# Patch transfers of sixteen channels, read-back in 4 KB pieces and a new order of work in an attention and expert-convolution kernel

## The chip, the cores and the metric

The kernel runs on one core of a Trainium2 chip. Its time is the device time of one launch in microseconds. A core has five engines with an instruction queue each, which run in order and wait for one another through semaphores: TensorE (PE, with its weight loads as PEld), VectorE (DVE), ScalarE (ACT), GpSimd (POOL) and SyncE (SP). SyncE issues nearly all transfers here; 16 DMA engines carry them out.

## The reference

The input x has 16 images of 256 channels and 64 x 64 pixels, in float32. Two residual layers follow one another.

```
h   = groupnorm(x)
q,k,v = w_qkv @ rmsnorm(h)              # 4 heads of 32
ctx = softmax_tokens(k) @ v^T           # 32 x 32 per head, over 4096 tokens
y   = x + rmsnorm(w_out @ (ctx @ softmax_channels(q)) + b_out)

h2  = groupnorm(y)
p   = softmax(router(mean(h2)) / 2)     # 4 experts, the best 2 per image
out = y + sum over the 2 experts e of
      p_e * (pw_e @ gelu(depthwise3x3_e(h2) + dw_b_e) + pw_b_e)
```

The gelu is the exact one, and pw_e is a 256 x 256 pointwise convolution. The experts differ per image, so each image's filters and pointwise weights are fetched after its routing.

## The kernel before

An image is cut into 8 groups of 512 tokens for the attention layer, and into 4 quarters of 16 rows (2 halves of 32) for the expert layer. Several images are in work at once: while image b is in its depthwise and pointwise stage, image b+1 goes through its output stage, and image b+2 is read and projected. "The next image" and "the one after" below mean these.

**The order.** `pipelined_path` writes all the work of the 16 images as rows, each a small function such as `out_norm(b, g, hf)` or `conv0(b, h, t)` with a place in time. The place is a start, plus a slot per group, plus an offset from a dictionary called PLAN of about 3,100 entries, in which a name such as "tap16@e1.2" overrides the common offset for certain images and groups. The rows are sorted by place (L1648) and emitted in that order under `tc.manual_schedule()` (L1649). So every engine's queue holds its instructions in the order of the rows; no scheduler moves them after that.

**The attention stage.** `turn_x` transposes tokens (PE, tile px), `x_keep` copies them scaled out of PSUM (ACT or DVE, tile xt), `project` makes q and k (PE, pq), `evacuate` takes the exponentials (ACT, e), `context` accumulates the contexts (PE, pc). Later `attend` computes the outputs (PE, po), `out_sq` their squares (ACT, junk), `out_norm` writes them scaled as tile ob (DVE at L1183, some on ACT at L1181), `out_turn` transposes ob (PE, tr, L1188), and `out_add` adds the result to the image in SBUF (DVE, ring, L1197).

**The expert stage.** Channels 128 to 255 are convolved on VectorE: `start1` on ACT (L1467), eight `tap1` on DVE (acc, L1474, 128 x 1024 each), `gelu1` on ACT (L1482). Channels 0 to 127 go through TensorE. `pad0` writes a padded half into pd; `lay` stores it to HBM (L1380); `spread` reads patches of it back into a tile xr, in which each partition holds one input row at one horizontal shift, for a block of 8 channels (L1393 and L1397); `conv0` multiplies them with banded filter tables (PE, dw, L1432), two calls `conv0(2v)` and `conv0(2v+1)` filling the same two PSUM banks. `gelu0` takes both banks to SBUF (ACT, hx, L1444), `put` stores them to HBM with channels and rows exchanged (L1449), and `take` reads them back with channels on partitions as tile hp (L1460). `pointwise` multiplies acc and hp with the experts' weights (PE, pw, L1503), `residual` adds the result to the image (DVE, ring, L1518), and `store` writes it out (L1521).

**Buffers.** There are four xr tiles of 8 channels, used in turn, three hx, three acc and one hp. PSUM's banks for dw, pw, px, tr and the others are handed out in turn in the order of the rows, so each first write to a bank waits for the last reader of its former contents.

Of the kernel before, what the change touches and what calls it, by code (L numbers as in the profile page):

```python
# [16 lines left out]
P = 128  # L17
# [7 lines left out]
NE = 4  # L25
# [25 lines left out]
NXR = 4  # L51
# [9 lines left out]
    "load_x1": 2.02, "mean": 1.19, "means": 13.36, "dev": 13.73, "devs": 17.34, "scale": 17.85,  # L61
    "bias": 21.91, "in_lead": 26.39, "norm0": -8.96, "norm1": -3.87, "turn_x0": 0.72, "x_sq0": 1.77,
    "x_sq1": 2.31, "turn_x1": 1.43, "x_sq2": 3.45, "x_sq3": 3.25, "token": 4.42, "x_keep0": 5.53,
    "x_keep1": 5.77, "x_keep2": 5.97, "x_keep3": 6.03, "project0": 3.18, "evacuate0": 6.05,
    "project1": 3.64, "evacuate1": 6.46, "project2": 3.67, "evacuate2": 6.47, "project3": 4.06,
    "evacuate3": 6.58, "context": 9.48, "q_sum": 8.22, "q_norm": 11.06, "q_turn": 14.73,
    "q_keep": 16.31, "mix_a": 9.53, "mix_turn": 10.09, "mix_v": 11.08, "mix_vv": 11.63,
    "mix_b": 11.82, "mix_out": 13.35, "mix_c": 13.91, "mix_lead": 16.02, "attend0": -1.14,
    "out_sq0": -0.04, "out_sq1": 0.35, "out_scale0": 0.42, "out_norm0": 1.58, "attend1": -0.28,
    "out_sq2": 1.31, "out_sq3": 1.37, "out_scale1": 3.18, "out_norm1": 4.28, "out_turn0": 5.64,  # L70
    "out_add0": 6.51, "sq_sums0": 8.92, "out_turn1": 6.16, "out_add1": 7.06, "sq_sums1": 9.17,
    "sums1": 9.6, "means1": 9.77, "scale1": 10.52, "router": 10.97, "route": 11.89, "choose": 13.68,
    "pick_taps": 21.03, "route_lead": 21.97, "weigh": 29.78, "pick_bias": 41.15, "pad1": -10.35,
    "start0": -0.53, "tap01": 1.33, "tap02": 1.57, "tap03": 1.59, "tap04": 1.87, "tap05": 2.54,
    "tap06": 4.55, "tap07": 4.74, "tap08": 6.14, "gelu10": 13.51, "start1": 1.94, "tap11": 3.52,
    "tap12": 8.13, "tap13": 8.14, "tap14": 8.54, "tap15": 9.95, "tap16": 12.84, "tap17": 13.06,
    "tap18": 14.42, "gelu11": 15.46, "pw00": 16.32, "pw01": 16.45, "pw02": 17.78, "pw03": 17.83,
    "pw10": 16.09, "pw11": 16.24, "pw12": 19.85, "pw13": 20.43, "residual00": 19.8,
    "residual01": 20.37, "store0": 32.19, "residual10": 22.5, "residual11": 23.44, "store1": 26.19,
    "in_first": 0.96, "in_more": 1.71, "q_first": 3.46, "out_first": 27.07, "out_more": 37.75,  # L80
    "q_less": 0.19, "load_a0": -17.62, "load_a1": -6.91, "load_b0": -15.96, "load_b1": -6.67,
    "stats0": -13.55, "stats1": -1.94, "load_weights": 58, "scale_weights": -7.03,
    "end_pw00": 135.48, "end_pw01": -49.35, "end_pw02": 69.96, "end_pw03": 337.87,
    "end_residual00": 3.29, "end_residual01": 66.1, "end_pw10": 115.56, "end_pw11": -47.98,
    "end_pw12": -196, "end_pw13": -114.87, "end_residual10": -13.43, "end_residual11": 88.85,
    "x_0": 0.99, "x_1": -0.21, "x_2": -0.19, "x_e1": 5.09, "x_e2": 4, "route_0": -3.83,
    "route_1": 0.32, "route_2": -0.55, "route_e1": -1.2, "route_e2": -0.21, "out_0": -5.81,
    "out_1": -0.4, "out_2": 0.09, "out_e1": -1.85, "out_e2": -0.87, "q_0": -7.21, "q_1": -2.22,
    "q_2": 0.4, "q_e1": -1.65, "q_e2": -0.57, "in_0": -22.93, "in_1": 7.98, "in_2": 2.65,
    "in_e1": -1.58, "in_e2": 0.28, "pw04": -112.48, "pw14": -23.18, "x_last": 16.71,  # L90
    "v_last": 15.93, "v_e1": 3.4, "tap18@e2.3": 12.73, "start0@e1.3": -0.55, "x_sq2@2.2": 2.88,
    "gelu11@e1.2": 17.06, "tap03@0.1": 1.97, "project0@0.0": 2.01, "out_norm1@2.7": 4.71,
    "out_sq1@e2.0": 0.64, "out_scale1@1.2": 2.19, "evacuate0@1.2": 5.17, "context@1.7": 8.38,
    "out_scale1@0.0": 4.74, "q_norm@0.0": 15.63, "out_turn0@1.4": 5.23, "token@2.1": 4.75,
    "project0@2.7": 3.47, "context@0.7": 8.6, "attend1@e1.3": -2.08, "out_norm1@1.1": 3.87,
    "context@2.1": 7.79, "q_norm@0.6": 12.94, "out_norm0@1.1": 1.4, "gelu11@e2.3": 13.29,
    "evacuate2@1.7": 6.62, "out_norm1@0.6": 4.18, "evacuate2@2.2": 6.81, "project0@2.3": 4.02,
    "token@2.2": 4.19, "norm0@0.0": -14.16, "q_sum@0.0": 10.99, "x_sq2@2.6": 2.62,
    "norm1@0.0": -4.28, "out_norm1@e1.1": 5.78, "x_sq2@1.2": 2.18, "tap04@e2.2": 2.29,
    "x_keep0@0.5": 6.43, "out_turn0@1.2": 5.58, "evacuate3@1.7": 8.13, "x_sq2@2.5": 2.77,  # L100
    "turn_x0@0.0": -3.93, "out_scale0@1.2": 2.15, "tap13@2.0": 6.26, "x_keep3@1.2": 6.99,
    "out_turn0@1.3": 4.82, "q_sum@e2.6": 8.44, "x_sq2@0.0": -1.29, "scale1@0.0": 11.1,
    "token@0.1": 2.33, "q_sum@1.5": 10.67, "q_sum@1.1": 7.71, "tap12@e1.1": 3.08,
    "x_keep1@0.1": 3.76, "evacuate2@1.6": 5.71, "q_sum@1.3": 8.05, "route@0.0": 12.55,
    "x_sq2@1.4": 2.43, "q_turn@0.2": 15.05, "bias@0.7": 26.53, "token@1.4": 3.4,
    "pick_taps@e1.0": 23.22, "out_add0@2.5": 6.36, "means@0.7": 10.61, "dev@e2.7": 6.55,
    "evacuate3@1.2": 6.52, "x_sq3@1.4": 3.12, "x_keep1@0.7": 6.49, "mix_v@0.7": 11.95,
    "token@1.1": 4.49, "tap17@e2.3": 11.87, "out_turn0@e1.1": 7.3, "token@0.2": 4.15,
    "q_sum@1.2": 9.02, "out_norm0@1.2": 4.52, "x_keep0@0.7": 6.45, "mix_b@e1.7": 12.79,
    "choose@1.0": 14.4, "project0@e1.7": 2.76, "tap07@e1.2": 8.15, "tap11@e1.2": 5.96,  # L110
    "means@1.7": 3.31, "token@1.3": 3.93, "q_sum@e1.6": 8.87, "tap12@e2.0": 8.3,
    "out_scale0@1.3": 2.06, "route@e1.0": 12.62, "pick_taps@2.0": 19.25, "out_turn0@1.0": 5.21,
    "scale@0.7": 20.54, "tap06@e1.0": 3.75, "out_turn1@e2.2": 8.74, "token@0.7": 3.73,
    "q_sum@e2.7": 9.96, "stats0@e2.5": -12.47, "out_turn0@1.5": 5.79, "token@1.6": 3.52,
    "q_turn@e2.1": 14.09, "out_norm1@e2.5": 4.67, "weigh@0.0": 26.02, "x_sq2@1.0": 3.24,
    "out_turn0@0.3": 5.99, "turn_x0@2.2": -1.78, "mix_b@0.7": 18.63, "out_scale1@e2.6": 2.5,
    "gelu11@e1.0": 17.52, "token@e2.7": 4.04, "context@1.2": 12.21, "q_sum@e2.0": 7.26,
    "tap01@e1.3": 1.63, "tap12@e2.2": 6.87, "x_sq2@1.6": 3.27, "load_a1@1.6": -5.34,
    "q_sum@0.1": 9.32, "q_sum@2.5": 8.88, "q_norm@0.2": 14.49, "tap13@e2.3": 7.37,
    "weigh@2.0": 30.01, "q_sum@e2.3": 12.37, "stats1@1.0": -3.82, "q_sum@1.0": 8.13,  # L120
    "project1@2.2": 5.8, "context@1.4": 11.54, "mean@1.7": -2.48, "tap03@e1.2": 2.37,
    "token@2.4": 4.54, "q_turn@e2.3": 15.48, "mix_b@1.7": 11.59, "out_sq3@e2.5": 1.73,
    "pick_bias@1.0": 35.23, "tap03@e1.3": 2.45, "out_norm1@0.7": 3.64, "choose@2.0": 14.28,
    "out_turn0@0.1": 5.13, "x_keep1@0.5": 6.47, "out_norm1@0.5": 4.68, "router@2.0": 11.05,
    "means1@e1.0": 10.29, "mean@0.7": 2.67, "project0@e2.7": 2.49, "x_keep0@1.7": 6.78,
    "context@1.3": 10.14, "router@0.0": 11.21, "tap17@e1.3": 13.61, "sq_sums1@0.7": 11.44,
    "x_sq1@1.4": 2.79, "x_keep0@1.1": 6.45, "context@0.4": 10.21, "project2@2.3": 0.53,
    "out_turn1@e1.6": 7.27, "project0@e1.5": 5.68, "turn_x0@e1.7": 0.11, "q_sum@e2.5": 11.2,
    "out_turn0@e1.6": 5.98, "out_turn0@e2.5": 5.25, "tap01@e1.2": -3.61, "evacuate3@0.0": 7.65,
    "tap02@e2.2": 1.4, "sq_sums1@e1.7": 7.95, "x_sq2@0.1": 1.36, "scale_weights@0.7": -14.32,  # L130
    "out_scale1@e2.5": 1.99, "tap14@e1.0": 9.68, "tap04@e2.1": 1.62, "out_turn1@2.2": 8.6,
    "tap12@e1.2": 6.98, "x_keep2@0.7": 7.73, "out_turn0@0.6": 5.19, "means1@e2.0": 9.88,
    "q_sum@e1.1": 9.48, "tap05@e1.2": 3.33, "out_sq3@1.4": 1.68, "x_sq2@e1.3": 3.34,
    "q_sum@2.2": 8.55, "tap01@1.0": 2.07, "context@1.1": 9.76, "scale1@2.0": 10.36,
    "x_sq2@e1.5": 2.62, "mix_c@0.7": 21.87, "context@2.2": 14.9, "x_sq2@1.7": 1.88,
    "out_scale0@e2.6": 0.89, "dev@1.7": 7.62, "tap16@e2.3": 11.2, "q_sum@0.2": 11.88,
# [686 lines left out]
def pipelined_path(ctx, tc, ring, st_0, wqkv, x, w_outT, b_out, g_out, router_wT, router_b, dw, dw_b, pwT, pw_b, out):  # L823
# [630 lines left out]
    def take(b, h, v, r):  # L1454

        if ("hp", b, h) not in live:
            new(work, [P, TOPK * QR, HC], "hp", b, h, bufs=1)
# [828 lines left out]
```

## Time and profile before

| | |
|---|---|
| median of 3 runs | 2675.81 us (2675.36 to 2690.78) |
| the profiled execution | 2665.43 us, of which its span is 2663.7 us |
| mean granted TensorE clock | 0.970 |
| TensorE, VectorE, ScalarE busy | 2404.0, 2244.2, 2072.5 us |
| first 267 us | pipeline fills; PE busy 210.1 us |
| 267 to 2414 us | PE busy 1998.5 of 2147 us |
| last 249 us | no new image comes in; PE busy 195.4 us, clock 0.90 |
| moved by DMA | 581.15 MB, 218 GB/s in the mean |

The span runs from the first to the last instruction of the profiled execution; the rest of that execution's time is before and after. Clock means the share of the full TensorE clock that was granted. An idle time in the profile stands before the instruction that ended it, together with what released it.

### The profile page before, as it was taken

The numbers are of one execution on the slowest core, as the hardware profiler recorded it, in microseconds if no ns is written. First come the engines' busy times: TensorE is split into PE (matmuls) and PEld (weight loads), VectorE is DVE, ScalarE is ACT, GpSimd is POOL, SyncE is SP. The second block draws the span as 40 slices with busy tenths as digits, with TensorE's granted clock in tenths as the row PEclk, the third lists the DMA queues.
The fourth block names the chain that finished last, engine by engine and source line by source line (L and its number), as shares of the span: only waits on it lengthen the run. The fifth ranks groups of instructions, "written<-read, shape, count | busy, mean of one in ns | idle before, by whom it ended". The sixth has DMA issues, their size and how long they took to land.

```text
span 2663.7 us, 50175 instructions
## 1 busy us (share of the span) xinstructions
PE 2404.0 (90%) x17204; PEld 1604.7 (60%) x17204; DVE 2244.2 (84%) x3489; ACT 2072.5 (78%) x4848; POOL 912.5 (34%) x1217
## 2 busy tenths in 40 slices
PE   6897999989899998989999898999989899997877
PEld 5675666656665665656666565666666566564433
DVE  6565789879988898989988898988888888889887
ACT  3588988878788888878888887988888788875632
POOL 4243343333333333334333243432333343433200
PEclk9998999999999999999999999999999999998999
DMA  4848788878778778777877887787877777866885
GB/s 145 103 127 224 227 230 233 232 226 242 221 226 238 227 236 247 228 227 228 232 228 240 240 240 222 230 235 228 247 216 222 222 206 209 232 186 197 227 226 176
DMA packets 410840, 581.15 MB, mean 218 GB/s; under 512 B 66000, under 2 KB 279504, under 8 KB 406480
## 3 DMA queue, kind: packets, MB, share of 16 engines
q1 hardware_dynamic: 377248, 575.36, 74.8%
q10 hardware_dynamic: 33328, 2.49, 1.6%
q8 instruction: 139, 2.28, 0.4%
q14 instruction: 125, 1.02, 0.1%
HBM read 402.49 MB, written 175.24 MB: 217 GB/s over the span
## 4 chain that ended last, share of the span: by engine, by line
PE 43%; DVE 21%; DMA 15%; ACT 8%; issue 6%; POOL 3%; SPq 3%; DVEq 0%; ACTq 0%; POOLq 0%
PE pw L1503 19%; DVE acc L1474 11%; PE pq L1066 7%; DMA hid<-hx 5%; PE pc L1084 4%; PE po L1160 4%; DMA hp<-hid 4%; PE dw L1432 3%; PE px L1035 2%; PE tr L1188 2%; DVE ring L1518 2%; DVE ob L1183 2%; DMA xr<-lay 2%; DVE ring L1197 2%; DMA lay<-pd 2%
## 5 line engine op out<-in xcount | busy, mean ns | idle before, releaser
L1474 DVE SCALAR_TENSOR_TENSOR acc<-pd,ds,acc 128x1024 f32<-128x1024 f32 x1024 | 1324.0, 1298 | 44.7 <-ACT acc L1467 26.2
L1503 PE MATMUL pw<-acc,ps 128*128 128x512 f32 x1024 | 496.5, 623 | 26.8 <-ACT acc L1482 24.4
L1066 PE MATMUL pq<-wqkv_n,xg 128*128 128x256 f32 x2048 | 487.5, 385 | 13.7 <-ACT e L1074 3.5
L1503 PE MATMUL pw<-hp,ps 128*128 128x512 f32 x1024 | 479.9, 604 | 18.4 <-DMA hp<-hid 15.5
L959 POOL TENSOR_SCALAR s<-ss 128x2 f32<-128x2 f32 x256 | 125.5, 490 | 1020.6 <-ACT junk L1168 1015.4
L1066 PEld LDWEIGHTS pq<-wqkv_n,xg 128*128 128x128 f32 x2048 | 383.1, 192 | 90.4 <-issue 19.1
L1503 PEld LDWEIGHTS pw<-acc,ps 128*128 128x128 f32 x1024 | 191.1, 199 | 229.9 <-issue 154.8
L1503 PEld LDWEIGHTS pw<-hp,ps 128*128 128x128 f32 x1024 | 189.2, 193 | 204.7 <-issue 196.5
L1042 ACT ACTIVATE jx<-px 128x256 f32<-128x256 f32 x512 | 196.3, 383 | 131.8 <-PE px L1035 122.4
L1160 PE MATMUL po<-mw,qt 128*128 128x256 f32 x1024 | 265.1, 389 | 9.9 <-DVE ring L1197 3.8
L1518 DVE SCALAR_TENSOR_TENSOR ring<-pw,bs,ring 128x512 f32<-128x512 f32 x248 | 180.8, 744 | 107.5 <-PE pw L1503 104.5
L1074 ACT ACTIVATE e<-pq,r 128x256 f32<-128x256 f32 x512 | 210.8, 477 | 58.8 <-PE pq L1066 45.0
L1197 DVE SCALAR_TENSOR_TENSOR ring<-tr,gout,ring 128x512 f32<-128x512 f32 x256 | 187.1, 746 | 81.2 <-PE tr L1188 75.9
L1084 PE MATMUL pc<-xt,e 128*128 128x257 f32 x1024 | 252.4, 389 | 2.5 <-ACT xt L1053 1.7
L960 POOL TENSOR_TENSOR s<-s,mhalf 128x2 f32<-128x2 f32 x256 | 243.7, 952 | 21.4
L1168 ACT ACTIVATE junk<-po 128x256 f32<-128x256 f32 x512 | 198.0, 387 | 60.9 <-PE po L1160 52.1
L1432 PE MATMUL dw<-xr,taps 55*32 55x128 f32 x8192 | 185.4, 283 | 61.7 <-DMA xr<-lay 30.0
L1188 PE MATMUL tr<-ident,ob 128*128 128x128 f32 x1024 | 162.1, 285 | 67.6 <-DVE ob L1183 46.4
L1160 PEld LDWEIGHTS po<-mw,qt 128*128 128x128 f32 x1024 | 186.0, 194 | 61.5 <-issue 22.0
L1432 PEld LDWEIGHTS dw<-xr,taps 55*32 55x32 f32 x8192 | 128.5, 108 | 147.0 <-issue 28.1
L1444 ACT ACTIVATE hx<-dw 128x512 f32<-128x512 f32 x256 | 148.4, 594 | 86.9 <-PE dw L1432 60.8
L1084 PEld LDWEIGHTS pc<-xt,e 128*128 128x128 f32 x1024 | 191.2, 195 | 33.2 <-issue 5.1
(146 smaller groups left out, 3533.4 us busy)
## 6 DMA issues: line engine op xcount, KB each, us to landing
xr<-lay SPq DMA_DIRECT2D x512, 197.6 KB
hid<-hx SPq DMA_DIRECT2D x256, 256.0 KB
hp<-hid SPq DMA_DIRECT2D x128, 512.0 KB
out<-ring SPq DMA_DIRECT2D x128, 512.0 KB
xa<-in_x SPq DMA_DIRECT2D x240, 256.0 KB
xb<-in_x SPq DMA_DIRECT2D x240, 256.0 KB
ring<-in_x SPq DMA_DIRECT2D x120, 512.0 KB
lay<-pd SPq DMA_DIRECT2D x32, 1188.0 KB
```

The lines of the kernel that those rows point to most:

```text
L960: nc.gpsimd.tensor_tensor(out_t, out_t, mhalf[:, :n], ALU.pow)
L1066: nc.tensor.matmul(pq, xg[:, k, c * P : (c + 1) * P], wqkv[:, k, : 2 * HID], start=(k == 0), stop=(k == KH - 1),)
L1074: nc.scalar.activation(live["e", b, g][:, c], live["pq", b, g, c // 2][:, c % 2], AF.Exp, scale=live["r", b, g][:, c : c + 1],)
L1084: nc.tensor.matmul(live["pc", b], live["e", b, g][:, c, HID:], xt[g % 2][:, c], start=(g == 0 and c == 0), stop=(g == NG - 1 and c == CG - 1),
L1160: nc.tensor.matmul(po[:, c], qt[:, n * P : (n + 1) * P], live["mw", b], start=True, stop=True)
L1168: nc.scalar.activation(junk[:, :C], live["po", b, g, hf][:, c], AF.Square, accum_out=ss[:, c : c + 1])
L1188: nc.tensor.transpose(tr[:, c * P : (c + 1) * P], live["ob", b, g, c // 2][:, c % 2, k * P : (k + 1) * P], ident,)
L1197: nc.vector.scalar_tensor_tensor(xin, live.pop(("tr", b, g, k)), gout[:, k : k + 1], xin, ALU.mult, ALU.add, accum_out=live["sm", b][:, 0, ...
L1432: nc.tensor.matmul(pair[r][g * 2 * QR : (g + 1) * 2 * QR, s * HC : (s + 1) * HC], taps[ks, CB * t + i].rearrange("p i x -> p (i x)"), stri ...
L1474: nc.vector.scalar_tensor_tensor(acc, pd1[j % 2][:, t // 3 : t // 3 + QR, t % 3 : t % 3 + W], live["ds", b][:, i, t : t + 1], acc, ALU.mul ...
L1503: nc.tensor.matmul(po, w, rhs, start=begin, stop=end)
L1518: nc.vector.scalar_tensor_tensor(xo, po, bs, xo, ALU.add, ALU.add)
```

## The change

Three things are done together.

1. **xr.** Two tiles of 16 channels take the place of four of 8. `spread(b, h, v)` fills one tile for `conv0(2v)` and `conv0(2v+1)`. It issues two DMAs, one of 48 partitions and one of 6, for each of two channel blocks, as before, but with runs of 8440 bytes instead of 4216, and it is called 4 times a half instead of 8. All bytes and matmuls are as before.
2. **hp.** The read-back tile changes from `[P, 4, 1024]` within one unbroken row to `[P, 4, 1024 + 4]`; the four unused elements behind each part keep a run from going on, so that `take` moves 4 KB pieces, four to a channel. The matmuls read the same values. The table of filter bands, which uses the same memory once at the start, is reshaped to fit.
3. **PLAN.** Of the 2,865 offsets with a name in both kernels, 2,774 have another value. The number of rows falls from 10175 to 10047, the 128 calls of `spread`.

```diff
+HR = QR // 2 * HC
-NXR = 4
+NXR = 2
...
-    xr = [const.tile([P, CB, SW], FP, name=f"xr_{i}") for i in range(NXR)]
+    xr = [const.tile([P, 2 * CB, SW], FP, name=f"xr_{i}") for i in range(NXR)]
...
-    def spread(b, h, t):
+    def spread(b, h, v):
-        n = CB * SW - 2
-        tile_t = xr[(h * NU + t) % NXR].rearrange("p c x -> p (c x)")
+        n = 2 * CB * SW - 2
+        tile_t = xr[v % NXR].rearrange("p c x -> p (c x)")
         for r in range(2):
-            c0 = r * P // 2 + CB * t
-            run = lays[h][:, c0 : c0 + CB].rearrange("u c x -> u (c x)")[:, :n]
+            c0 = r * P // 2 + 2 * CB * v
+            run = lays[h][:, c0 : c0 + 2 * CB].rearrange("u c x -> u (c x)")[:, :n]
...
-        pair, x = live["dw", b, h, v], xr[(h * NU + t) % NXR]
+        pair, x = live["dw", b, h, v], xr[v % NXR][:, n * CB : (n + 1) * CB]
...
-            new(work, [P, TOPK * QR, HC], "hp", b, h, bufs=1)
+            new(work, [P, 2 * TOPK, HR + 4], "hp", b, h, bufs=1)
...
-            out=live["hp", b, h][cs].rearrange("c k x -> c (k x)"), in_=hids[h][cs]
+            out=live["hp", b, h][cs, :, :HR], in_=hids[h][cs].rearrange("c (s n) -> c s n", n=HR)
...
-                rhs = hp[:, i * QR + rows.start : i * QR + rows.stop, j % NB2 * W : (j % NB2 + 1) * W]
+                rhs = hp[:, 2 * i + q, :HR].rearrange("p (r x) -> p r x", x=HC)
+                rhs = rhs[:, :, j % NB2 * W : (j % NB2 + 1) * W]
...
-            for t in range(NU):
-                at("c", b, h, f"spread{t}", spread, b, h, t)
+            for v in range(NU // 2):
+                at("c", b, h, f"spread{2 * v}", spread, b, h, v)
```

In the middle images, the same in each of them, the new order differs from the old mainly in these places:

- On VectorE the second `out_norm` of an even group stands after the sixth tap of the accumulator in work, where it stood after the eighth. The statistics of a new image's groups stand ahead of a residual instead of behind it.
- On TensorE the rows around the start of a half come as conv0, conv1, turn_x0, turn_x1, context, pointwise, conv2, conv3, pointwise; before, they came as conv0, conv1, turn_x0, pointwise, conv2, turn_x1, conv3, context, pointwise. The `project` calls of a group come as 0, 2, 1, 3.
- On SyncE the fourth `spread` of a half comes before the fetch of pointwise weights.
- As the rows set the PSUM bank of each tile, some first writes follow another reader than before.

## The prediction

> **What bounds the kernel now.** I read the page first: its busy rows, then the shares of the chain.
>
> ```profile
> span 2663.7 us, 50175 instructions
> ...
> PE 2404.0 (90%) x17204; PEld 1604.7 (60%) x17204; DVE 2244.2 (84%) x3489; ACT 2072.5 (78%) x4848; POOL 912.5 (34%) x1217
> ...
> PE 43%; DVE 21%; DMA 15%; ACT 8%; issue 6%; POOL 3%; SPq 3%; DVEq 0%; ACTq 0%; POOLq 0%
> ```
>
> TensorE is busy 90% of the span. The change removes no matmul, no tap, no activation and no byte, so at most the other 260 us can shrink, plus what matmuls lose at a lower clock. The next view, TensorE's waits by releaser, says what the 260 us are made of.
>
> ```profile
> PE tr L1188 <- DVE ob L1183: 46.4, 29, 4.1
> PE dw L1432 <- DMA xr<-lay: 30.0, 29, 4.3
> ...
> PE dw L1432 <- DVE ob L1183: 16.0, 8, 2.3
> PE pw L1503 <- DMA hp<-hid: 15.5, 14, 2.1
> ```
>
> The columns are total, count and longest. The two transfers that the change reshapes, xr and hp, hold 45.5 us. VectorE's `out_norm` (tile ob) holds 62.4 us, and these depend on the order of work alone. By stretches of the span, xr waits are 4.2 us before 333 us, 12.2 us from 333 to 2414 (4.4, 0.6 and 7.2) and 13.6 us in the last 250; hp waits are 9.9 us in the middle and 5.6 at the end.
>
> In the middle an image takes 157.3 us, from its first wait for hp (1216.83) to that of the next (1374.12). TensorE's timeline in that image shows two stalls of over a microsecond:
>
> ```profile
> 1319.11 0.69 PE L1188 MATMUL tr<-ident,ob 128*128 128x128 f32 x2 [3.87 <-DVE ob L1183]
> ...
> 1340.90 1.04 PE L1432 MATMUL dw<-xr,taps 55*32 55x128 f32 x30 [2.24 <-DVE ob L1183]
> ```
>
> The stall in brackets stands before the instruction. What matters next is the granted clock behind them (columns: length, busy time of PE, PEld, DVE, ACT and POOL, then clock, DMA share, GB/s):
>
> ```profile
> 1319.10:1321.00 1.90, 1.89 (x4) 1.16 (x5) 1.83 (x6) 0.72 (x1) 0.00 (x0) 0.50 0.91 221
> ...
> 1341.00:1343.50 2.50, 2.50 (x58) 1.79 (x66) 0.00 (x0) 0.41 (x2) 0.00 (x0) 0.51 0.91 267
> 1343.50:1346.50 3.00, 3.00 (x34) 2.13 (x19) 0.00 (x0) 2.90 (x8) 1.27 (x2) 0.84 0.57 157
> ```
>
> Both stalls are followed by some microseconds at half clock. The dw stall comes 8 times, once in each of eight middle images.
>
> **Part 1: the order laid out anew.** Conv2 of half 1 takes a PSUM bank that `out_norm(2,1)` of the next image has to read first. VectorE stands so:
>
> ```profile
> 1335.79 4.46 DVE L1474 SCALAR_TENSOR_TENSOR acc<-pd,ds,acc 128x1024 f32<-128x1024 f32 x3
> 1340.17 0.69 DVE L1183 TENSOR_TENSOR ob<-po,s 128x512 f32<-128x512 f32 x1
> ```
>
> Three taps of 1.3 us stand in front of the `out_norm`. In the changed order two of them stand behind it, so it ends 2 x 1.3 = 2.6 us earlier. On TensorE the changed order puts turn_x1, the context matmuls and a pointwise part ahead of conv2, which comes about 2.2 us later in it. The stall needed 2.24 us and gets 4.8: it goes, with 2.5 us to spare. The same early `out_norm` of group 4 removes a stall of 0.43 us at 1240.16. The two taps that are now later feed `gelu1` and a pointwise part; their accumulator is finished after the same number of instructions as before, so nothing is late by more than the 0.69 us of the one that overtook.
>
> The clock loss behind the dw stall is 2.5 x 0.49 + 3.0 x 0.16 = 1.7 us of full-clock work. Here a rule can be set against the row. The Trainium skill, "TensorE: Matmul & The Clock Gate", Part 1, has the clock fall to half only after an idle window of some 3.4 us, and its closing table asks only for no gaps over about 3 us. By that rule a stall of 2.24 us costs no clock, and the part is worth 8 x (2.24 + 0.43), about 20 us by the eight stalls' sum (16.0 + 3.4 = 19.4). By the row the clock was 0.51 after it, and the part is worth 19.4 + 8 x 1.7 = 33.0 us. I take the row; the rule's 19.4 is the lower end.
>
> The 3.87 us stall at 1319.11 I leave in place. It closes a stretch of VectorE from its wait for a pointwise result (1262) to the `out_norm` at 1318.4, 57 us of the same operations in both orders. If the images come faster, this stretch still follows its pointwise result at the same distance. If it shrank by half with its clock loss (about 2.9 us), another 8 x 3.4 = 27 us would go; that is the upper end of this part.
>
> **The wait that the order adds.** The changed order has `out_turn(3,1)` of the next image take a bank that ScalarE's `x_keep` of group 4 must empty. In the trace of before TensorE reaches this turn at 1365.44, and the nearest ScalarE row is
>
> ```profile
> 1367.02 1.54 ACT L1053 ACTIVATE xt<-px,r 128x256 f32<-128x256 f32 x4
> ```
>
> of which the two that count end at 1367.85: a stall of up to 2.4 us. ScalarE idled 3.62 us at 1343.09 for a transpose that now comes earlier, and 1.30 us at 1364.22 for the load of xb. With most of this idle time gone the stall is 0 to 2.4 us. I take 0.7, x 8 = +5.6 us. Behind the turn stand the pointwise matmuls of quarter 3, for which VectorE's residual and then its next stretch wait; that is why it would count in full.
>
> **Part 2: sixteen channels in a transfer.** `spread` issues two DMAs per 8 channels, at these prices on SyncE (minimum, median, maximum, in ns):
>
> ```profile
> L1393 SPq DMA_DIRECT2D xr<-lay x512: 565/579/1706, 214.0 to 2617.5; - x171
> L1397 SPq DMA_DIRECT2D xr<-lay x512: 704/717/1202, 214.7 to 2618.2; - x171
> ```
>
> Half of both go: 256 x (579 + 717) ns = 332 us of SyncE's time. SyncE's queue is in order, with L1460's `take`, L1449's `put` and the loads behind these issues, but it has 2664 us and waits itself for others most often, so only what was late because of it counts. Of the xr waits in the middle (about 1.0 us each, 30.0 over 29) I let 0.6 us in each go: the pair's last issue is 1.3 us earlier, and the landing later by 0.7 us. That 0.7 is an estimate: at 233 GB/s and a DMA share of 0.80 one of the 16 engines carries 18.2 GB/s, and three runs of 8.4 KB instead of 4.2 KB take 1.4 instead of 0.7 us. This gives 12.2 x 0.6 = 7 us. Of hp's 9.9 us I let 4 go, since a take is issued up to 1.3 us earlier. Together -11 us; the ends are 0 (the issues were hidden) and -22 (all of these waits go).
>
> Against it stands that the first conv of a pair now waits for all 16 channels, and that the tile is free only when conv(2v-3) has read it, where before it was conv(t-4). In the middle there is room: from conv(2v-3) to conv(2v) TensorE has 9.5 to 11.2 us of work (before 11.3 to 12.3), against 1.3 us of issue plus about 3.5 of landing. In the last two images the room shrinks to 3.0 to 9.8 us, and there each of 16 pairs may be 0.7 us late. I take half, +6 us with the start of the first image; the ends are 0 and +20.
>
> **Part 3: hp in 4 KB pieces.** The page counts 410840 packets, 406480 of them under 8 KB: the 4096 runs of 16 KB of 128 takes lie within the rest, so they do travel whole, and the change cuts them. The trace has no read back in 4 KB pieces. Above: a take lands 5.7 to 9.4 us after its issue, of which the bytes alone are 1.8 us (two runs of 16 KB per engine at 18.2 GB/s); [...] 1 us less at the 14 late ones is worth -14 us. Below: the Trainium skill, "DMA: Bandwidth & Descriptors", Rules for kernel authors, speaks against it: join small transfers into large ones. If each landed 1 us later, that is +14 to +20 us. The nearest rows, xr's 4.2 KB runs, land in 2.6 to 7.2 us and are no slower for their size. I take 0. The same page's formula, 2.0 us plus bytes over 436 GB/s, would make the larger xr transfer only 0.45 us later than the smaller; with it Part 2's +6 would be +4. I keep the row's 0.7.
>
> **The sum.** -33.0 (order) + 5.6 (new wait) - 11 (waits for transfers) + 6 (ends) + 0 = -32.4 us on the profiled execution's 2665.4 us (span 2663.7 and 1.7 around it), so 2633 us. The median of the runs shown is 10.4 us above that execution; carried over, the forecast is 2643 us, or 1.2% less. A measurement of this kernel can tell about 1% from no change.
>
> **Rivals.**
> *The stall changes place.* The new bank wait takes its full 2.4 us, or VectorE's 57 us stretch sets the period whatever stands around it. For it: VectorE is busy 139 of 157 us, and its longest idle time is one of 6.3 us at 1347.10, for a pointwise result. Against it: that wait itself follows TensorE, behind the removed stall. Then parts 2 and 3 remain: about 2676 - 11 + 6 = 2671 us.
> *Transfers too coarse.* Two tiles are refilled only as wholes. SyncE waits 161.4 us for VectorE's statistics and 108.4 us for stores; when it stands in such a wait while a tile is free, a whole pair is late. There are 128 pairs. From 0.25 us a pair the gain is gone, and from 0.5 us the kernel is over 1% slower. At 0.6 us a pair, half clock behind it included, it is +77 - 32: 2720 us. Against it are the windows of 9.5 to 11.2 us above.
> *More than forecast.* The 3.87 us stall shrinks too and all waits of the middle go: 2643 - 27 - 11 = 2605 us.
> *It doesn't do what it says.* Pieces of 4 KB that land as before, issues that were hidden: the order alone remains, 2643 + 11 - 6 = 2648 us, inside the forecast's own range.
>
> **How the numbers follow.** Forecast with the case of hidden issues 0.50 (2620 to 2665), more 0.08, stall in another place 0.25, too coarse 0.17. About nine tenths of the first two lie below 2649, and the rest of them with the third within 1%, allowing for a third case that misses: faster 0.54, same 0.28, slower 0.18. The range 2602 to 2697 leaves out the worse half of the coarse case.
>
> **What would show it.** In the profile after: no wait of dw for ob of 2 us in the middle images; a period near 153 to 154 us; clock 0.98 or more in the mean; xr issues 256 + 256; waits of tr for ACT xt under 1 us each. Wrong would be: xr waits on TensorE well above 30 us, tr waiting for xt or for ob longer than now, or the period still 157 us.

## The result, and the profile after

The changed kernel took 2755.75 us (median of 4 runs, 2750.68 to 2759.08) against 2680.28 us for the kernel before in the same series. The ratio is 1.0275, with a 95% interval from 1.0235 to 1.0314: slower, where 2643 us had been forecast. The profiled execution has a span of 2757.4 us and a granted clock of 0.953 (before: 0.970).

The page of the changed kernel, first its busy row, then the first queue's share of the DMA engines' time, then the shares of the chain that ended last:

```profile
PE 2432.8 (88%) x17204; PEld 1636.1 (59%) x17204; DVE 2233.3 (81%) x3489; ACT 2075.4 (75%) x4848; POOL 858.8 (31%) x1215
...
q1 hardware_dynamic: 370848, 575.45, 79.9%
...
PE 39%; DMA 34%; DVE 11%; ACT 9%; issue 3%; SPq 2%; POOL 1%; DVEq 0%; ACTq 0%; POOLq 0%
```

The span grew by 93.7 us. TensorE does the same matmuls in 28.8 us more (2404.0 to 2432.8), at the lower clock, and idles 64.9 us more. DMA's share of the chain went from 15% to 34%, VectorE's from 21% to 11%. The bytes of q1 are the same, but its packets occupy 79.9% of a longer span: 2203 us an engine, before 1992.

TensorE's waits in the changed kernel (total, times, longest):

```profile
PE dw L1431 <- DMA xr<-lay: 89.6, 44, 4.1
PE pw L1503 <- DMA hp<-hid: 42.8, 23, 7.2
PE tr L1187 <- DVE ob L1182: 24.7, 11, 3.2
PE tr L1187 <- DVE ring L1196: 16.5, 10, 2.7
...
PE tr L1187 <- ACT xt L1052: 10.4, 12, 2.5
...
PE po L1159 <- ACT xt L1052: 6.1, 8, 2.7
```

The 62.4 us that TensorE waited for `out_norm` have shrunk to 27.8 (24.7 in front of tr, and 3.1 in front of dw, where none is as long as 2 us). In their place xr has gone from 30.0 to 89.6 us and hp from 15.5 to 42.8. Its timeline in a middle image shows where:

```profile
1071.41 0.38 PE L1431 MATMUL dw<-xr,taps 55*32 55x128 f32 x2 [1.74 <-DMA xr<-lay]
1074.55 1.96 PE L1431 MATMUL dw<-xr,taps 55*32 55x128 f32 x62 [2.76 <-DMA xr<-lay]
```

These are the first matmuls of conv4, the start of the third pair: its two channel blocks arrive one after the other, and each is waited for. Averaged over the images from the fifth to the thirteenth, the period is 162.9 us instead of 158.4, counted between the first hp matmuls of images.

The trace also has every packet with its size and duration. Runs of 4216 and 8440 bytes occur in xr's transfers only, so these can be followed alone (108 packets to a group of four issues, taken in order of time; medians; the third row counts from the end of the last issue, the fourth from the start of the first). A group carries 455 KB before and 911 KB in the changed kernel:

```
                             before       changed
channels per group           8            16
packet, mean                 242 ns       629 ns      (17.4 and 13.4 GB/s)
last issue to last packet    2.05 us      6.8 us
first issue to last packet   4.9 us       9.7 us
```

### The profile page after: what moved, and what is told of

Its sections match the earlier page's. It is cut to its first block, busy times and chain, and to the rows that moved or that the text cites. A ratio compares the mean times of both kernels' runs of the same rounds, so it can differ in the third digit from the quotient of the medians.

```text
span 2757.4 us, 49308 instructions
## 1 busy us (share of the span) xinstructions
PE 2432.8 (88%) x17204; PEld 1636.1 (59%) x17204; DVE 2233.3 (81%) x3489; ACT 2075.4 (75%) x4848; POOL 858.8 (31%) x1215
## 3 DMA queue, kind: packets, MB, share of 16 engines
q1 hardware_dynamic: 370848, 575.45, 79.9%
## 4 chain that ended last, share of the span: by engine, by line
PE 39%; DMA 34%; DVE 11%; ACT 9%; issue 3%; SPq 2%; POOL 1%; DVEq 0%; ACTq 0%; POOLq 0%
PE pw L1503 15%; DMA xr<-lay 11%; DMA hp<-hid 6%; PE pq L1065 6%; DMA hid<-hx 6%; DVE acc L1473 5%; PE po L1159 4%; PE pc L1083 4%; PE dw L1431 3%; DMA ring<-in_x 3%; PE tr L1187 3%; DMA out<-ring 2%; PE px L1034 2%; DMA xa<-in_x 2%; DMA lay<-pd 2%
## 5 line engine op out<-in xcount | busy, mean ns | idle before, releaser
L1503 PE MATMUL pw<-hp,ps 128*128 128x512 f32 x1024 | 484.4, 609 | 47.3 <-DMA hp<-hid 42.8
L958 POOL TENSOR_SCALAR s<-ss 128x2 f32<-128x2 f32 x256 | 115.1, 450 | 1125.4 <-ACT junk L1167 1122.5
L1431 PE MATMUL dw<-xr,taps 55*32 55x128 f32 x8192 | 192.3, 291 | 115.6 <-DMA xr<-lay 89.6
L1159 PE MATMUL po<-mw,qt 128*128 128x256 f32 x1024 | 275.1, 399 | 12.2 <-ACT xt L1052 6.1
L1431 PEld LDWEIGHTS dw<-xr,taps 55*32 55x32 f32 x8192 | 137.2, 111 | 199.4 <-issue 84.7
L1073 ACT ACTIVATE e<-pq,r 128x256 f32<-128x256 f32 x512 | 212.0, 476 | 38.7 <-PE pq L1065 26.6
L959 POOL TENSOR_TENSOR s<-s,mhalf 128x2 f32<-128x2 f32 x256 | 227.7, 889 | 21.3
L1159 PEld LDWEIGHTS po<-mw,qt 128*128 128x128 f32 x1024 | 192.3, 201 | 64.4 <-issue 22.5
L1187 PE MATMUL tr<-ident,ob 128*128 128x128 f32 x1024 | 169.9, 299 | 67.0 <-DVE ob L1182 24.7
L1187 PEld LDWEIGHTS tr<-ident,ob 128*128 128x128 f32 x1024 | 131.8, 152 | 131.9 <-DVE ring L1196 33.0
```

Source lines behind the costliest of these rows:

```text
L959: nc.gpsimd.tensor_tensor(out_t, out_t, mhalf[:, :n], ALU.pow)
L1073: nc.scalar.activation(live["e", b, g][:, c], live["pq", b, g, c // 2][:, c % 2], AF.Exp, scale=live["r", b, g][:, c : c + 1],)
L1159: nc.tensor.matmul(po[:, c], qt[:, n * P : (n + 1) * P], live["mw", b], start=True, stop=True)
L1187: nc.tensor.transpose(tr[:, c * P : (c + 1) * P], live["ob", b, g, c // 2][:, c % 2, k * P : (k + 1) * P], ident,)
L1431: nc.tensor.matmul(pair[r][g * 2 * QR : (g + 1) * 2 * QR, s * HC : (s + 1) * HC], taps[ks, CB * t + i].rearrange("p i x -> p (i x)"), stri ...
L1503: nc.tensor.matmul(po, w, rhs, start=begin, stop=end)
```

## The experiments

Every kernel was timed beside the kernel before on the same chip; ratios are against that. The kernel before took 2669 to 2674 us in these series and 2680 us in that of the result, so a difference in us between kernels of different series can be some 10 us off, and the ratios are the better measure. Where rows are left out or a tap is missing, the quoted expectation says so.

**The parts of the change, one at a time.** `x16_alone` has only the first part of the change, `hp4_alone` only the second. `order_alone` has the new PLAN and neither of the others. `two_by_eight` is the changed kernel with each tile filled by two transfers:

```diff
 # two_by_eight, in spread
+        for m in range(2):
+            o = m * CB * SW
             for r in range(2):
-                run = lays[h][:, c0 : c0 + 2 * CB]...[:, :n]
+                run = lays[h][:, c0 : c0 + CB]...[:, :n]      # c0 with m * CB added
-                    out=tile_t[k0 : k0 + 3 * QR, :n],
+                    out=tile_t[k0 : k0 + 3 * QR, o : o + n],
 # order_alone, in the list of rows
+                at("c", b, h, f"spread{t // 2 * 2}", spread, b, h, t)
```

> The old order and the old hp, with the two tiles of 16 channels and their transfers alone; each spread stands where the first of its two old ones stood. Transfer theory (the longer runs are what costs): in the profile of the changed kernel a pair's last packet ends 6.8 us after its last issue, before 2.05 us; TensorE's waits for xr go from 30 to about 90 us and the time to 2730 to 2770 us. Order theory (the new order is what costs): xr waits stay near 30 us and the time within 1% of 2680 us.

Measured: 2760.91 us, ratio 1.0342 (1.0320 to 1.0365). The transfers, with their two tiles and their places, cost 89 us in the old order. The last packet ends 6.1 us after the last issue. TensorE's own waits for xr rose only from 30.0 to 41.2 us, so most of the loss is not in the row where it was expected. SyncE's waits show part of it:

```profile
SPq L978 <- ACT xg L1027: 131.8, 45, 8.0
...
SPq L1449 <- ACT hx L1444: 110.0, 62, 6.7
...
SPq L1449 <- ACT junk L1168: 94.1, 27, 6.1
...
SPq L851 <- DMA xr<-lay: 55.1, 40, 1.9
```

Before, these were 83.2, 63.1, 14.6 and 0.2 us. The last is a load of an image that stands until an xr transfer has landed, though it needs nothing of it. In the trace nearly every issue of SyncE (1760 of 1770) has the completion semaphore of the eighth issue ahead of it, so a late transfer also holds what stands eight places behind.

> The old order and the old xr, with hp read back in 4 KB pieces alone. Transfer theory: the pieces move no faster than the 16 KB ones (both at 13 to 15 GB/s an engine in the two profiles), so 2670 to 2695 us. A rival in which the 4 KB pieces cause the late hp (TensorE's waits for hp went from 15.5 to 42.8 us) gives 2700 us or more.

Measured: 2672.94 us, ratio 1.0009 (0.9994 to 1.0024). The pieces of 4 KB make no difference. In its trace the 16384 added packets of 4096 bytes take 294 us an engine, where the 4096 of 16 KB took 284.

> The new order with the old transfers: four tiles of 8 channels, hp in 16 KB pieces; the two old spreads stand together at the place of the new one. Transfer theory: the prediction's order part holds by itself, 2640 to 2670 us, with no 2 us wait of dw for ob. Order theory: 2740 us or more.

Measured: 2716.61 us, ratio 1.0173 (1.0154 to 1.0192). Both expectations miss: the order neither gains nor carries the whole loss. Its waits:

```profile
PE pw L1502 <- DMA hp<-hid: 72.3, 27, 6.6
PE tr L1187 <- DVE ob L1182: 27.1, 12, 3.4
...
PE dw L1431 <- DMA xr<-lay: 17.6, 24, 3.0
```

The patches come in time here and the read-back comes late. ScalarE's `gelu0` in one half shows why (hx is one of three buffers, free when `put` has stored it):

```profile
1039.19 0.60 ACT L1443 ACTIVATE hx<-dw 128x512 f32<-128x512 f32 x1 [2.73 <-DMA hid<-hx]
1046.14 0.60 ACT L1443 ACTIVATE hx<-dw 128x512 f32<-128x512 f32 x1
1049.58 0.60 ACT L1443 ACTIVATE hx<-dw 128x512 f32<-128x512 f32 x1 [0.78 <-DMA hid<-hx]
1053.08 0.60 ACT L1443 ACTIVATE hx<-dw 128x512 f32<-128x512 f32 x1 [1.19 <-DMA hid<-hx]
1055.17 0.60 ACT L1443 ACTIVATE hx<-dw 128x512 f32<-128x512 f32 x1 [0.62 <-DMA hid<-hx]
```

Four of the five wait for a store. In the new order the third spread stands between the two puts of the first pair; SyncE issued 8 spread DMAs from 1040.41 to 1046.07, and the next put came at 1046.16.

> The changed kernel, but each tile of 16 channels is filled by two transfers of 8 (runs of 4216 bytes); tiles, order and hp stay. If the length of a run costs: the last packet comes about 2 us after the last issue again, 2680 to 2700 us. If two tiles that are free only as wholes cost (the rival of coarse transfers): 2740 us or more, with xr waits of TensorE near 90 us still.

Measured: 2731.02 us, ratio 1.0229 (1.0205 to 1.0252). The last packet comes 1.9 us after the last issue, and 7.65 us after the first of the eight issues, though these take 5.65 us; the four issues of the changed kernel take 2.9 us and their last packet comes 9.7 us after the first. So half as many issues deliver the same bytes 2 us later. TensorE's xr waits are 14.8 us, so two tiles that are free only as wholes do not make xr late in this order. The time is between the two expectations, and hp is now the late one, with waits of 81.7 us. By the ratios it is 0.5% below the changed kernel, and the two intervals overlap.

**The order further.** `early_norm` takes one move out of the new order and makes it in the old one; `early_spread`, `order_early8`, `order_puts` and `after_puts` move spreads in the new one.

```diff
 # early_norm, after rows.sort, for each second out_norm of an even group
+        late = [m for m in range(n - 60, n) if m >= 0 and rows[m][4] is tap1][-2:]
+        ...                                  # these two rows go directly behind the out_norm
 # early_spread, order_early8
+                ...                          # spread v = 2, 3 goes directly behind conv(2v - 3)
 # order_puts, after_puts
+                ...                          # spread v = 2, 3 goes behind both puts of pair v - 2
```

> The kernel before with one thing moved: the last two taps of an accumulator stand behind the second out_norm of groups 0, 2, 4 and 6, where they stood in front. This is the prediction's part 1 alone. By its row (stall and half clock) 2672 - 33 = about 2640 us; by the clock rule alone 2652 us; if VectorE's stretch sets the period and the stall only changes place, 2665 to 2680 us, with another wait of TensorE in the place of dw for ob (16 us).

Measured: 2692.67 us, ratio 1.0099 (1.0063 to 1.0135). The wait of dw for ob is gone (16.0 to 0) and the kernel is 1% slower. In the same part of an image TensorE now shows

```profile
1167.23 5.41 PE L1066 MATMUL pq<-wqkv_n,xg 128*128 128x256 f32 x16 [1.87 <-DVE ring L1197]
...
1175.49 0.44 PE L1188 MATMUL tr<-ident,ob 128*128 128x128 f32 x2 [2.63 <-DVE ob L1183]
...
1210.06 0.38 PE L1432 MATMUL dw<-xr,taps 55*32 55x128 f32 x2 [2.20 <-DMA xr<-lay]
1211.37 0.67 PE L1432 MATMUL dw<-xr,taps 55*32 55x128 f32 x30 [0.94 <-DMA xr<-lay]
```

where before it had 3.87 for ob and 2.23 for ob. Conv2 no longer waits for VectorE, but conv7 of the same half waits 3.1 us for its patches (the last two lines), and the projection waits 1.87 us for VectorE. In total xr waits rose by 16.0 us and pq's waits for ring by 12.0 (2.9 to 14.9). The stall changed place, and more than that.

> The changed kernel with the third and fourth spread of each half moved to directly behind conv1 and conv3, where their tile comes free; the puts of the first pair then stand behind them. If the place of the spread in SyncE's queue costs: TensorE's waits for xr fall from 90 to under 45 us and the time to 2700 to 2730 us. If the transfer itself costs wherever it stands (the longer runs, and lost DMA time of 211 us an engine): 2745 us or more.

Measured: 3069.5 us, ratio 1.1493 (1.1448 to 1.1537), against both expectations. A spread that stands at the head of SyncE's queue until conv3 is done holds the puts behind it; with three hx buffers ScalarE then stops, and TensorE behind it:

```profile
PE tr L1187 <- ACT hx L1443: 168.0, 18, 10.7
```

> The new order with the old transfers, and the spreads of the third and fourth pair behind conv1 and conv3. If the new order loses only because its spreads stand in front of the puts when SyncE has twice the issues (hp waits of 72 us in the run without the move): hp waits fall below 35 us, 2640 to 2680 us. If the order itself is slower elsewhere: 2700 us or more.

Measured: 2953.9 us, ratio 1.1090 (1.1050 to 1.1129), for the same reason (139.3 us in the same row). These two runs tell how much hangs on SyncE's order, not what the new order lacks.

> The new order with the old transfers (2717 us), with the spreads of the third and fourth pair behind the two puts that they stood in front of; the old order has its puts in front in the same way. If the puts waiting behind the spreads' issues are what makes hp late there (TensorE's hp waits 72 us): hp waits below 40 us, 2660 to 2690 us. If the new order loses elsewhere (its waits for ring and xt, and takes that stand behind other puts): 2705 us or more.

Measured: 2732.72 us, ratio 1.0226 (1.0205 to 1.0247). hp waits fell from 72.3 to 40.1 us and xr waits rose from 17.6 to 82.9. SyncE's time was only handed from one to the other. The expectation is not quite right on the old order: there the first of the third pair's two spreads stood in front of the puts.

> The changed kernel with the same move. With 16-channel transfers that land 9.7 us after their first issue, a later spread makes xr later than the puts gain: 2755 to 2800 us, xr waits above 90 us. If the puts matter more than the spreads: below 2740 us.

Measured: 2779.46 us, ratio 1.0398 (1.0376 to 1.0420), with xr waits of 112.6 us, as the first expectation has it. The changed kernel's own place for its spreads is better than the two that were tried.

**What sets the pace.**

> The kernel before without the last of VectorE's eight taps; the convolution of channels 128 to 255 lacks it. VectorE has 128 x 1.3 = 166 us less to do. If VectorE's stretch between a pointwise result and the out_norm sets the images' pace, as the failed move of out_norm suggests, the time falls by more than 50 us. If TensorE sets it and the 2.2 and 3.9 us stalls are its only waits for VectorE: at most 60 us of stalls can go, less what comes in their place, so 2630 us or more.

Measured: 2659.07 us, ratio 0.9957 (0.9943 to 0.9971). VectorE is busy 2091.9 us, 152 less than before, and the kernel gains 14 us. Neither expectation names the reason, but the second holds in size. TensorE waits 15.6 us less for `out_norm` (tr for ob 46.4 to 38.3, dw for ob 16.0 to 8.5), 12.2 us less for `gelu1`'s acc, and 12.5 us more for xr. VectorE's stretch doesn't set the pace.

**The transfers of 6 partitions, and SyncE's issues.**

```diff
 # no_six (changed kernel), before_no_six, x16_no_six: the second issue of spread is left out
-            nc.sync.dma_start(
-                out=tile_t[k0 + 3 * QR : k0 + WK, :n],
-                in_=bass.AP(run.tensor, run.offset + QR * su, [[1, 3], [su, 2], run1]),
-            )
 # before_one54, after_one54: one transfer, and the table's rows in its order
-                out=tile_t[k0 : k0 + 3 * QR, :n],
-                in_=bass.AP(run.tensor, run.offset, [[su, QR], [1, 3], run1]),
+                out=tile_t[k0 : k0 + WK, :n],
+                in_=bass.AP(run.tensor, run.offset, [[su, WR], [1, 3], run1]),
-                    k = 3 * QR + 2 * dx + u - QR
+                    k = 3 * u + dx
```

> The changed kernel without the transfers of 6 partitions; the patches' last two rows are left out, so the depthwise sums lack them. If these transfers hold a few DMA engines (their outer dimension is 3, and TensorE's xr waits end on them in 43 of 44 cases): the last packet ends 2 to 3 us after the last issue instead of 6.8, and the time is below 2710 us. If long runs are slow by themselves: 5 us or more, and 2735 us or more.

Measured: 2629.17 us, ratio 0.9849 (0.9816 to 0.9882), 4.1% below the changed kernel by the two ratios. But the last packet still ends 7.0 us after the last issue, and long runs move at 12.5 GB/s an engine: the time is as the first theory has it, the packets as the second. From the first issue they end 1.5 us earlier, 8.25 us.

> The kernel before without its transfers of 6 partitions; the last two rows of the patches are left out, so the depthwise sums lack them. In the changed kernel this was worth 125 us. If SyncE's issues bound both kernels, it is worth about the same or more here (512 issues less): 2570 us or below. If the old order hides them: 2645 to 2672 us.

Measured: 2571.74 us, ratio 0.9629 (0.9612 to 0.9645). The old order hides them little better: it gains 98 us, or 3.7%. TensorE's waits for xr fall to 3.9 us, for hp to 3.7 and dw's for ob to nothing, 53.9 us in all; the rest came with a higher clock (0.974; 26.6 us less busy time) and smaller waits.

> The old order with the 16-channel transfers alone (2761 us), without the transfers of 6 partitions; the patches' last two rows are left out, so the depthwise sums lack them. Beside the kernel before without them (2572 us) it differs only in the run length, the number of issues and the tiles. If the long runs lose mainly through the transfers of 6 partitions: within 1.5% of 2572 us. If a burst of long runs is late by itself: 2630 us or more.

Measured: 2627.99 us, ratio 0.9842 (0.9817 to 0.9866), 56 us or 2.2% above `before_no_six`. So the coarser transfers cost 56 us without the 6 partitions too, and 89 us with them (2761 against 2672). Run length, number of issues and tiles are changed together here, and these runs do not separate them.

> The kernel before, 8 channels as ever, but the patches of a block come in one transfer of 54 partitions (18 rows by 3 shifts) in place of 48 and 6; the filter table has its rows in the same new order. SyncE loses 512 issues of 0.72 us (367 us in all), bytes and run length stay. If the issues were hidden, as part 2 of the prediction has it but for 11 us: 2650 to 2675 us. If SyncE's queue is what sets the images' pace: below 2640 us. If 18 rows spread worse over the DMA engines than 16: 2690 us or more.

Measured: 2628.93 us, ratio 0.9862 (0.9815 to 0.9909). This version leaves nothing out and beats both kernels: 41 us below before, and 4.0% below the changed one by the two ratios (0.9862 over 1.0275). Its only transfer of a block costs SyncE 752 ns in place of 579 + 717, so SyncE saves 512 x 0.544 = 279 us:

```profile
L1393 SPq DMA_DIRECT2D xr<-lay x512: 731/752/2065, 214.5 to 2575.9; - x171
```

And that although a block's last packet now ends 6.9 us after its first issue instead of 4.9. That the saved issues are what gained is the likely reading, not one that a run shows by itself.

> The changed kernel with one transfer of 54 partitions in place of 48 and 6. The run without the 6-partition transfers took 2629 us, 125 less than the changed kernel, at the same rate of the long runs. If that gain came from two issues less per pair (1.4 us of SyncE and two completions to wait for): below 2700 us here too. If it came from the bytes left out (11% of them) and from the engines that carry them: 2740 us or more.

Measured: 2759.66 us, ratio 1.0343 (1.0303 to 1.0383): nothing gained. With long runs the last packet ends 11.2 us after the first issue, and TensorE's xr waits rise to 110.4 us.

> The changed kernel, its transfers of 48 partitions with runs of 8440 bytes, those of 6 partitions in two of 8 channels each. Bytes per engine are those of the changed kernel, issues are two more per pair. If a long run queued on few engines is what makes these late: below 2730 us. If SyncE's issues and the total rate in a burst (160 GB/s for xr, in every kernel alike) decide: 2750 us or more.

Measured: 2728.28 us, ratio 1.0215 (1.0196 to 1.0234), with two issues more per pair. That is 27 us below the changed kernel by the medians, but 0.6% or 16 us by the ratios. TensorE's xr waits fall to 64.2 us. Shortening the runs of the 6 partitions alone recovers between a fifth and a third of the change's loss.

> The kernel before with the two issues of a block exchanged: 6 partitions first, then 48. Issues, bytes and run lengths stay. If the 6-partition transfers are late because a few engines carry them behind their share of the 48, their start 0.6 us earlier brings 2650 to 2665 us; if only their issues and bytes cost, 2665 to 2680 us.

Measured: 2699.55 us, ratio 1.0103 (1.0077 to 1.0128), outside both expectations: 1% slower.

> The changed kernel with the same exchange. Six partitions in shorter runs brought 27 us here (2728). If it is their place behind 8440-byte runs that costs, this brings about as much: 2715 to 2740 us, with TensorE's xr waits below 75 us. If not: 2745 to 2765 us.

Measured: 2751.82 us, ratio 1.0291 (1.0265 to 1.0316), no change. The place of the smaller transfer behind the larger is not what costs.

## Why the prediction was wrong

**The step that failed first is the 0.7 us of Part 2, and with it the term of -11 us.** It let a pair's transfer land 0.7 us later, from three runs of 8.4 KB per engine. That is one of the four DMAs of a group. All four carry 911 KB, are issued within 2.9 us and go through the same engines. At the 18.2 GB/s an engine that the prediction took, they would need 3.1 us; measured are 7.4 us from the first packet to the last. Sums over the packets show what became of them (medians over all bursts of a trace; a burst runs from its first xr packet to its last; the last two rows count the packets of every transfer in that time):

```
                       two_by_eight   changed    before_no_six   x16_no_six
length of a run        4216 B         8440 B     4216 B          8440 B
bytes of a burst       911 KB         911 KB     405 KB          810 KB
its issues take        5.65 us        2.9 us     1.2 us          1.2 us
first to last packet   6.0 us         7.4 us     2.4 us          5.5 us
rate of xr             153 GB/s       123 GB/s   166 GB/s        148 GB/s
engines' time taken    70%            100%       102%            102%
rate of all transfers  199 GB/s       228 GB/s   243 GB/s        206 GB/s
```

(A share over 100% means that records of packets overlap.) In `two_by_eight` the issues set the pace: 911 KB in 5.65 us are 161 GB/s, and the engines have time left. In the changed kernel the issues are over early and the engines are full until the last packet, 9.7 us after the first issue. Full engines, moreover, moved long runs more slowly than short ones, as the last two columns show. So the 160 GB/s "in every kernel alike" of one expectation is not a limit of the engines: it is near the pace of the issues in `two_by_eight`.

The end of a burst is long besides. The last quarter of the packets takes 3.1 us in the changed kernel, 1.5 us in `two_by_eight`, and 1.7 us where the transfers of 6 partitions are left out (no_six). Between 2.0 and 0.7 us before the end only three xr packets are in flight in the median, where the middle half of a burst has 15. So the transfers of 6 partitions end it. Their place in the queue is not the reason (after_six_first); their run length has a part (six_by_eight). Full engines are not the only way to be late, either: in after_one54 packets take up 78% of the engines' time, and the last one comes 11.2 us after the first issue.

So the 332 us of SyncE's issues did go, and the gain was lost to the engines: the term of -11 us was in truth +89 us in the old order (x16_alone), and about +27 us in the new one (1.0275 for the changed kernel against 1.0173 for order_alone). The middle was said to have room, 9.5 to 11.2 us of TensorE's work against about 4.8 us; the transfer alone takes 9.7. The formula that the prediction quotes from the Trainium skill ("DMA: Bandwidth & Descriptors"), with 0.45 us, was further off than the 0.7 us. How much of the 89 us is the length of the runs and how much the tiles and the places of the spreads stays open: no run fills tiles of 16 channels by short runs in the old order.

**The second step that failed is the -33 us of Part 1.** What was said of the queues came true: the dw stall went (it is that of conv2 in an image's first half), in the changed kernel, in `order_alone` and in `early_norm`, and in the first two nearly half of tr's waits for ob went with it. But removing a wait is worth its length only if nothing else arrives at the same time. early_norm, with the prediction's move alone, was 23.5 us slower; seven_taps, with 152 us less for VectorE, gained 14. The patch round trip (lay, spread, conv, gelu, put, take) weighed more than TensorE's 45.5 us of recorded waits for it tell: leaving out part of it was worth 98 us. The prediction read the size of the lever from the waits' table, where only the last of several late arrivals is named. The clock's row was read rightly, and the Trainium skill's rule that was set against it ("TensorE: Matmul & The Clock Gate", Part 1) does not fit: in `early_norm`, without the stall, the clock in the 2.6 us behind conv2's start is 1.00 in each of five middle images, where it was 0.51 behind a stall of 2.24 us. But the loss comes back with the stalls that take the place of the old ones: the mean is 0.953 after, where 0.98 was expected.

The new order by itself costs 45 us with the old transfers. With the new transfers the same order is no loss (1.0275 against 1.0342 in the old order), so the two costs don't add: 89 and 45 us apart, 75 us together. That the third spread between two puts suits a SyncE with half the issues would fit this, but is not shown. Which part of the order costs the 45 us stays open; moving the spreads past the puts handed the wait from hp to xr.

**The new bank wait** was there, at 10.4 us for tr, 6.1 for po and 3.3 for pw, all behind xt: 19.8 us, where 5.6 were taken and 8 x 2.4 = 19 was the upper end. Not all of it is the order's: tr waited 8.2 us for xt in x16_alone, in the old order, and 4.1 us in order_alone.

**Part 3** was right: 0 taken, 1.0009 measured. The Trainium skill's rule that was set against it ("DMA: Bandwidth & Descriptors", Rules for kernel authors) speaks of small transfers, and these pieces lie within one of 512 KB.

**The rivals.** "Too coarse" gave 2720 us and had 0.17. Its size per pair was near: xr waits rose by 59.6 us over 128 pairs, 0.47 us each, before clock and hp. Its mechanism, tiles that are refilled only as wholes, was not what the new order shows: `two_by_eight` has the same two tiles, and its xr waits are 14.8 us. In the old order it is untested. The sign came from the term that was priced at -11 us and the one at +6 beside it, and none of the rivals asked what the DMA engines do with a burst twice as dense.

## What to carry to other kernels

Fewer, larger transfers take away issue time, and with it a pacing that spreads the load; before counting that as a gain, divide all the bytes of a burst by the rate that whole bursts reach in the trace, compare this with the time that the issues took, and look whether that rate was the engines' or only the issues' pace (70% and 100% of the engines' time here). An engine's table of waits names the last arrival only; a chain of transfers through an in-order queue can be nearly as late in many places, and then a stall elsewhere is worth little. Here fewer issues paid with the runs left short: one transfer of 54 partitions in place of 48 and 6 gained 1.4%.

## What the runs showed of the hardware

- A packet of 4216 bytes took 242 ns in the mean (median 164) in the kernel before, one of 8440 bytes 629 ns (median 627) in the changed kernel: 2.6 times as long for twice the bytes. In the single transfers of 54 partitions they took 217 and 495 ns.
- In the middle half of a burst 11 xr packets were in flight before and 15 in the changed kernel, but 9 with single transfers of 54 partitions, at either run length.
- A transfer of 18 rows by 3 shifts lands its last packet 5.1 us after its last issue, where 16 rows by 3 and 2 by 3 beside it take 2.05 us, at the same run length. The bursts last 3.6 and 3.3 us; the difference is mainly the start, 3.7 us after the first issue instead of 1.5.
- Exchanging the two issues of a block in SyncE's queue, at the same bytes and runs, made the kernel before 1.0% slower (six_first) and left the changed one as it was (after_six_first).
- The clock was 0.74 in the 4 us around xr stalls of 1.74 and 2.76 us:

```profile
1071.00:1075.00 4.00, 0.82 (x22) 0.61 (x29) 0.45 (x1) 2.70 (x6) 0.00 (x0) 0.74 0.72 149
```
